# A two-layer interaction network: first tile loaded and multiplied in pieces, first leftovers behind tile 1, layer 2's weights loaded later, matmuls on ones meanwhile

## The chip, the cores and the metric

One core of one Trainium2 chip. The metric is device microseconds of one launch. The kernel before takes 2290.15 us, the median of 3 runs (2289.32 to 2290.17).

## The reference

```python
ROWS, FIELDS, EMB = 4096, 32, 16
def _cin_layer(out, x, W, b, gamma, beta):
    h = jnp.einsum('rne,rfe->rnfe', out, x).reshape(r, -1, e)   # all products of two fields
    h = jnp.einsum('rce,oc->roe', h, W) + b[None, :, None]
    return _batchnorm(h, gamma, beta)                            # statistics over rows and e
h1 = _cin_layer(x, x, W1, b1, g1, beta1)                         # W1: 128 x 1024
out, direct1 = h1[:, :64], h1[:, 64:]
direct2 = _cin_layer(out, x, W2, b2, g2, beta2)                  # W2: 128 x 2048
y = jnp.concatenate([direct1, direct2], axis=1).sum(axis=-1)
```

All in fp32. Layer 2 can't start before the statistics of the whole of layer 1 are there.

## The kernel before

Layer 1 works on 128 tiles of 512 sites. For each tile two factors, a and b (128 x 1024 each, 512 KB), are loaded; VectorE forms four blocks of products, z; TensorE multiplies each with a block of weights. Products that don't fit this pattern ("leftovers", zr, from a load r) serve eight tiles at a time and enter as the first matmuls of every fourth tile. The weights are the sum of two loaded parts. ScalarE evicts, VectorE takes statistics.

```python
w1_sb = wpool.tile([P, 6, P], FP, tag="w1", name="w1_sb")
nc.scalar.dma_start(w1_sb, w1)
w1m_sb = lpool.tile([P, 6, P], FP, tag="a", name="w1m_sb")
nc.scalar.dma_start(w1m_sb, w1m)
bn_sb = load_bn()
w2_sb = const.tile([P, 16, P], FP, tag="w2", name="w2_sb")
nc.scalar.dma_start(w2_sb, w2)                       # 1 MB, used only in layer 2
...
for t in range(NT):
    s = t % GROUP
    if s == 0:
        r = load_rem(t // GROUP)
        zr = rpool.tile([P, T], FP, tag="zr", name="zr")
        nc.vector.tensor_tensor(zr, r[:, :T], r[:, T:], ALU.mult)
    a, b = load_main(t)                              # lpool: three buffers of a and of b
    z = zpool.tile([P, 2, 2, T], FP, tag="z", name="z")     # two buffers
    nc.vector.tensor_tensor(z, a..., b..., ALU.mult)
    if s % 4 == 0:
        for k in range(4):
            ps = pss[t + k] = psum.tile([P, T], FP, tag="ps", name="ps")
            rows = slice(32 * k, 32 * (k + 1))
            nc.tensor.matmul(ps, w1_sb[rows, 4 + s // 4, :], zr[rows, :], start=True, stop=False)
    for m in range(4):
        nc.tensor.matmul(pss[t], w1_sb[:, m, :], z[:, m // 2, m % 2, :], start=False, stop=(m == 3))
    if t > 0:
        finish(t - 1)                                # evictions and statistics
```

A scheduler orders each engine's queue when the kernel is built; it is not always the order of the text.

## Time and profile before

| | before |
|---|---|
| time, median of 6 runs | 2289.79 us |
| first tile's first product on TensorE | 13.41 us |
| eviction of tile 3 | 30.29 us |
| last eviction of layer 1 | 495.34 us |
| TensorE idle between the layers | 16.2 us |

The evictions are the clock by which this study reads layer 1: they come as TensorE finishes a tile. When TensorE never waits, the last eviction comes 465.05 us after tile 3's (495.34 - 30.29), so **any excess over 465.05 is time that TensorE lost after tile 3**.

### The profile page before, as it was taken

The numbers are of one execution on the slowest core, as the hardware profiler recorded it, in microseconds if no ns is written. First come the engines' busy times: TensorE is split into PE (matmuls) and PEld (weight loads), VectorE is DVE, ScalarE is ACT, GpSimd is POOL, SyncE is SP. The second block draws the span as 40 slices with busy tenths as digits, with TensorE's granted clock in tenths as the row PEclk, the third lists the DMA queues.
The fourth block names the chain that finished last, engine by engine and source line by source line (L and its number), as shares of the span: only waits on it lengthen the run. The fifth ranks groups of instructions, "written<-read, shape, count | busy, mean of one in ns | idle before, by whom it ended". The sixth has DMA issues, their size and how long they took to land.

```text
span 2288.8 us, 15238 instructions
## 1 busy us (share of the span) xinstructions
PE 2245.0 (98%) x5376; PEld 982.4 (43%) x5376; DVE 1750.0 (76%) x1129; ACT 398.7 (17%) x580; POOL 2.3 (0%) x5
## 2 busy tenths in 40 slices
PE   8999999979999999999999999999999999999997
PEld 3444444434444444444444444444444444444443
DVE  6888888877777777777777777777777777777776
ACT  3555555556000000000000000000000000000000
POOL 0000000000000000000000000000000000000000
PEclk9999999989999999999999999999999999999998
DMA  8888888868888888888888888888888888888883
GB/s 316 298 305 295 298 292 301 296 201 158 153 150 151 153 154 155 155 150 151 153 157 155 154 150 151 152 158 154 154 150 151 152 159 154 154 149 151 152 155 92
DMA packets 132428, 417.05 MB, mean 182 GB/s; under 512 B 14848, under 2 KB 14848, under 8 KB 115456
## 3 DMA queue, kind: packets, MB, share of 16 engines
q1 hardware_dynamic: 131616, 413.20, 81.7%
q10 hardware_dynamic: 736, 2.89, 0.4%
q8 instruction: 42, 0.69, 0.1%
q14 instruction: 34, 0.28, 0.0%
HBM read 278.66 MB, written 3.15 MB: 123 GB/s over the span
## 4 chain that ended last, share of the span: by engine, by line
PE 77%; issue 22%; DVE 0%; ACT 0%; POOLq 0%; ACTq 0%; DVEq 0%
PE ps L211 77%; ACT h L177 0%; DVE mv L60 0%; POOLq L276 0%; ACTq L182 0%; DVE d L224 0%; DVEq L276 0%; ACT e L213 0%; DVE stats L214 0%; DVE d L215 0%; DVE ss L72 0%; DVE c L69 0%; ACT sd L64 0%; DVE r L66 0%; DVE ss L75 0%
## 5 line engine op out<-in xcount | busy, mean ns | idle before, releaser
L211 PE MATMUL ps<-z,w_sb 128*128 128x512 f32 x4096 | 1761.1, 593 | 16.2 <-ACT h L177 16.2
L208 DVE TENSOR_TENSOR z<-a,b 128x2048 f32<-128x2048 f32 x512 | 1173.0, 2291 | 446.4 <-PE ps L211 439.5
L211 PEld LDWEIGHTS ps<-z,w_sb 128*128 128x128 f32 x4096 | 779.2, 190 | 998.1 <-issue 980.8
L163 PE MATMUL ps<-z,w_sb 128*128 128x512 f32 x1024 | 450.9, 598 | 3.2 <-DVE z L151 3.2
L213 ACT ACTIVATE e<-ps,bn_sb 128x512 f32<-128x512 f32 x128 | 87.9, 687 | 1635.0 <-PE ps L211 1624.0
L151 DVE TENSOR_TENSOR z<-a,b 128x2048 f32<-128x2048 f32 x128 | 293.4, 2292 | 68.9 <-PE ps L163 65.0
L163 PEld LDWEIGHTS ps<-z,w_sb 128*128 128x128 f32 x1024 | 193.0, 191 | 259.6 <-issue 251.0
L129 ACT ACTIVATE e<-ps,bn_sb 128x512 f32<-128x512 f32 x128 | 87.9, 687 | 219.5 <-PE ps L163 219.5
L214 DVE BATCH_NORM_STATS2 stats<-e 128x6 f32<-128x512 f32 x128 | 87.7, 685 | 5.3 <-ACT e L213 5.3
L132 DVE BATCH_NORM_STATS2 stats<-e 128x6 f32<-128x512 f32 x128 | 87.8, 686 | 3.4 <-ACT e L129 3.4
L130 ACT ACTIVATE ed<-ps,bn_sb 64x512 f32<-64x512 f32 x128 | 87.4, 683 | 3.2
L131 ACT ACTIVATE h<-ps,bn_sb 64x512 f32<-64x512 f32 x128 | 87.2, 681 | 2.4
L215 DVE TENSOR_REDUCE d<-e 128x32 f32<-128x512 f32 x128 | 85.5, 668 | 0.0
L177 ACT ACTIVATE h<-h,keep 128x512 f32<-128x512 f32 x64 | 45.7, 800 | 3.8 <-issue 1.9
L161 PE MATMUL ps<-zr,w_sb 32*128 32x512 f32 x256 | 37.4, 655 | 8.1 <-DVE w_sb L115 8.1
L135 DVE TENSOR_REDUCE d<-ed 128x32 f32<-128x512 f32 x64 | 42.8, 668 | 0.0
L161 PEld LDWEIGHTS ps<-zr,w_sb 32*128 32x128 f32 x256 | 10.2, 186 | 31.7 <-issue 23.5
L148 DVE TENSOR_TENSOR zr<-r 128x512 f32<-128x512 f32 x16 | 10.9, 682 | 6.7 <-DMA r<-in_xr 6.7
L60 DVE BATCH_NORM_AGGREGATE mv<-stats 128x2 f32<-128x768 f32 x2 | 7.2, 3612 | 0.0
L129 ACT ACT_TABLE_LOAD x1 | 1.3, 1283 | 8.5 <-DMA bn_sb<-in_bn 8.5
L224 DVE TENSOR_SCALAR d<-d,ss 128x2048 f32<-128x2048 f32 x2 | 2.6, 1343 | 0.0
L180 POOL TENSOR_SCALAR d<-d,direct 128x2048 f32<-128x2048 f32 x1 | 2.0, 2048 | 503.3 <-DVE direct L174 503.3
(17 smaller groups left out, 6.7 us busy)
## 6 DMA issues: line engine op xcount, KB each, us to landing
b<-in_xb SPq DMA_DIRECT2D x128, 1024.0 KB, 7.2
a<-h SPq DMA_DIRECT2D x512, 256.0 KB, 5.2
a<-in_xa SPq DMA_DIRECT2D x128, 512.0 KB, 4.9
b<-in_xb SPq DMA_DIRECT2D x128, 512.0 KB, 5.6
r<-in_xr SPq DMA_DIRECT2D x16, 512.0 KB, 6.1
out<-d SPq DMA_DIRECT2D x2, 1024.0 KB, 4.5
w_sb<-in_w ACTq DMA_DIRECT2D x1, 1024.0 KB, 10.0
out<-d ACTq DMA_DIRECT2D x2, 512.0 KB, 8.9
```

Source lines behind the costliest of these rows:

```text
L129: nc.scalar.activation(e, ps, AF.Identity, bias=b1)
L130: nc.scalar.activation(ed[to, :], ps[KEEP:, :], AF.Identity, bias=b1[KEEP:])
L131: nc.scalar.activation(hs[c][to, :], ps[:KEEP, :], AF.Identity, bias=b1[:KEEP])
L132: nc.vector.bn_stats(stats1[:, t, :], e)
L151: nc.vector.tensor_tensor(z, a.rearrange("p (a t) -> p a t", a=2).unsqueeze(2).to_broadcast([P, 2, 2, T]), b.rearrange("p (b t) -> p b t", ...
L161: nc.tensor.matmul(ps, w1_sb[rows, 4 + s // 4, :], zr[rows, :], start=True, stop=False)
L163: nc.tensor.matmul(pss[t], w1_sb[:, m, :], z[:, m // 2, m % 2, :], start=False, stop=(m == 3))
L208: nc.vector.tensor_tensor(z, a.unsqueeze(1).to_broadcast([P, 4, T]), b, ALU.mult)
L211: nc.tensor.matmul(ps, w2_sb[:, m, :], z[:, k, :], start=(m == 0), stop=(m == 15))
L213: nc.scalar.activation(e, ps, AF.Identity, bias=b2)
L214: nc.vector.bn_stats(stats2[:, t, :], e)
L215: nc.vector.tensor_reduce(d2[half][:, c * RT : (c + 1) * RT], e.rearrange("p (r e) -> p r e", e=EMB), AX.X, ALU.add,)
```

## The change

It is meant to let TensorE start sooner and at full clock: the bytes of the first products come first, and matmuls on ones keep TensorE busy until they land.

```diff
+STARTERS = 3
+LATER = 6
+        ones = zpool.tile([P, 2, 2, T], FP, tag="z", name="ones")[:, 0, 0]
+        nc.vector.memset(ones, 1.0)
+        started = psum.tile([P, T], FP, tag="ps", name="started")
+        for _ in range(STARTERS):
+            nc.tensor.matmul(started, ones[:, :P], ones, start=True, stop=True)
         w1_sb = wpool.tile([P, 6, P], FP, tag="w1", name="w1_sb")
-        nc.scalar.dma_start(w1_sb, w1)
-        w1m_sb = lpool.tile([P, 6, P], FP, tag="a", name="w1m_sb")
-        nc.scalar.dma_start(w1m_sb, w1m)
+        w1m_sb = wpool.tile([P, 6, P], FP, tag="w1m", name="w1m_sb")
+        a0, b0 = factors()
+        load_a(nc.sync, a0, 0, 0, 1)          # first half of a
+        load_b(nc.scalar, b0, 0, 0, 1)        # first half of b
+        load_w1(0, 1)                         # first block of both parts of the weights
+        load_b(nc.sync, b0, 0, 1, 1)
+        load_a(nc.sync, a0, 0, 1, 1)
+        load_w1(1, 6)
...
-        nc.scalar.dma_start(w2_sb, w2)
-        nc.vector.tensor_tensor(w1_sb, w1_sb, w1m_sb, ALU.add)
+        add_w1(0, 1)
...
+            if t == 0:
+                r = load_rem(0)
+                multiply(z, a, b, range(1), range(1));    main(t, z, range(1), True, False)
+                add_w1(1, 6)
+                multiply(z, a, b, range(1), range(1, 2)); main(t, z, range(1, 2), True, False)
+                multiply(z, a, b, range(1, 2), range(2)); main(t, z, range(2, 4), True, False)
+                continue
+            if t == 1:
+                for half in range(2):
+                    multiply(z, a, b, range(half, half + 1), range(2))
+                    main(t, z, range(2 * half, 2 * half + 2), True, False)
+                zr = multiply_rem(r)
+                leftover(0, 2)                # leftovers of tiles 0 to 3, formerly first of all
+                finish(0)
+                continue
...
+            evicted = finish(t - 1)
+            if t == LATER:
+                with tc.issue_after(evicted.ins):
+                    nc.scalar.dma_start(w2_sb, w2)
```

(Cut; some calls are joined on a line. Layer 1's matmuls are also chained in the order of the text, a tile's a and b now stand ahead of r in it, and the second part of the weights, w1m_sb, no longer takes one of the three buffers of a.)

## The prediction

> **What bounds the kernel now.** I read the page's costliest groups first, to learn which engine is never waited out of layer 1.
>
> ```profile
> L163 PE MATMUL ps<-z,w_sb 128*128 128x512 f32 x1024 | 450.9, 598 | 3.2 <-DVE z L151 3.2
> ...
> L151 DVE TENSOR_TENSOR z<-a,b 128x2048 f32<-128x2048 f32 x128 | 293.4, 2292 | 68.9 <-PE ps L163 65.0
> ...
> L161 PE MATMUL ps<-zr,w_sb 32*128 32x512 f32 x256 | 37.4, 655 | 8.1 <-DVE w_sb L115 8.1
> ```
>
> Layer 1's 1024 matmul records waited 3.2 us in all, once, at the start; VectorE waited 65 us for TensorE. So from the first product on, layer 1 is bound by TensorE. Each program matmul is two records, so a tile is 8 records. The timeline of the first 40 us, read second, shows what comes before that steady state, and the evictions (ScalarE, output e) give the pace:
>
> ```profile
> 0.73 0.39 SPq L92 DMA_DIRECT2D r<-in_xr  x1
> 0.74 0.41 ACTq L108 DMA_DIRECT2D w_sb<-in_w  x1
> ...
> 2.14 0.70 ACTq L113 DMA_DIRECT2D w_sb<-in_w  x1
> ...
> 8.14 2.09 PE L161 MATMUL ps<-zr,w_sb 32*128 32x512 f32 x8 [8.14 <-DVE w_sb L115]
> ...
> 11.06 2.29 DVE L151 TENSOR_TENSOR z<-a,b 128x2048 f32<-128x2048 f32 x1 [2.97 <-DMA b<-in_xb]
> ...
> 13.41 16.84 PE L163 MATMUL ps<-z,w_sb 128*128 128x512 f32 x32 [3.17 <-DVE z L151]
> ...
> 17.84 0.34 PEld L163 LDWEIGHTS ps<-z,w_sb 128*128 128x128 f32 x1 [0.52 <-issue]
> 18.69 0.34 PEld L163 LDWEIGHTS ps<-z,w_sb 128*128 128x128 f32 x1 [0.52 <-issue]
> 19.36 0.19 PEld L163 LDWEIGHTS ps<-z,w_sb 128*128 128x128 f32 x1 [0.33 <-issue]
> 19.79 0.19 PEld L163 LDWEIGHTS ps<-z,w_sb 128*128 128x128 f32 x1 [0.24 <-issue]
> ...
> 19.99 0.69 ACT L129 ACTIVATE e<-ps,bn_sb 128x512 f32<-128x512 f32 x1 [10.24 <-PE ps L163]
> ...
> 23.42 0.69 ACT L129 ACTIVATE e<-ps,bn_sb 128x512 f32<-128x512 f32 x1 [1.34 <-PE ps L163]
> ...
> 34.99 0.69 ACT L129 ACTIVATE e<-ps,bn_sb 128x512 f32<-128x512 f32 x1 [2.60 <-PE ps L163]
> ```
>
> Columns are start, duration, engine, and in brackets the idle time before. Four things are to be seen. TensorE does nothing until 8.14 and no product of tile 0 until 13.41, because b lands only at 11.06. Weight loads then come every 0.85 us until about 19.4 and every 0.43 us after it: seven records at half speed, which cost 7 x 0.427 = 3.0 us. Tile 0 is done at 19.97 and tile 1 at 23.40, 3.43 us apart; where a tile has leftovers (30.29 to 34.99) it is 4.70. Last, the evictions of layer 1 end like this:
>
> ```profile
> 495.34 0.69 ACT L129 ACTIVATE e<-ps,bn_sb 128x512 f32<-128x512 f32 x1 [1.34 <-PE ps L163]
> ```
>
> 19.99 + 96 x 3.434 + 31 x 4.70 = 495.4. So nothing but TensorE's own time passes between tile 0 and layer 1's end: whatever TensorE gains by tile 1 should be kept to the end of layer 1, and layer 2 hangs on that end by the batch norm (495.3 to the first matmul at 511.5). Lastly the DMA over the first 12 us, in 40 slices of 0.3 us:
>
> ```profile
> GB/s 0 0 0 0 0 68 109 150 123 246 276 393 393 444 416 396 403 434 440 410 424 435 371 385 494 356 533 410 341 464 478 341 423 437 341 492 410 355 410 410
> ```
>
> Bytes flow from 1.5 us, at about 410 GB/s from 3.3 us: the start is bound by transfers. Summed, 0.66 MB are in by 4.2 us, 1.8 MB by 7.0, 3.4 MB by 10.8. Ahead of b or beside it stood r, both weight sets of layer 1 and the 1 MB of layer 2's weights.
>
> **What the Trainium skill says.** "TensorE: Matmul & The Clock Gate", section "What's actually happening": the array runs at half clock until it has been busy for a whole free-running window of about 3.4 us, and falls back after an idle one. The trace agrees: 0.853 against 0.43 us per record, the fast pace reached 5.9 us after the first product, and layer 2, after 16.2 us idle, starts slow again:
>
> ```profile
> 511.00:512.00 1.00, 0.46 (x1) 0.49 (x2) 0.44 (x1) 1.00 (x3) 0.00 (x0) 0.50 0.83 188
> ...
> 517.00:518.00 1.00, 1.00 (x2) 0.32 (x2) 0.00 (x0) 1.00 (x3) 0.00 (x0) 0.75 0.98 197
> 518.00:519.00 1.00, 1.00 (x4) 0.51 (x3) 0.79 (x1) 1.00 (x3) 0.00 (x0) 1.00 0.72 100
> ```
>
> (Per microsecond, the third column from the end is the granted clock. Around 15 us it reads 1.00, against the matmuls' own pace there; I trust the pace.) "VectorE: DVE Perf Modes", the section on the TRN2 errata: an fp32 product takes (N+151)/0.96 ns; the trace's 2292 ns for N=2048 agrees, so 512 columns cost 0.69 us and 1024 cost 1.22. "DMA: Bandwidth & Descriptors", section "Issuing engines are not separate DMA queues": loads issued from two engines share the same 16 DMA engines. The trace agrees: b waits behind w2 of the other queue. So only the order of the bytes can help, not the second queue.
>
> **The change part by part.**
> 1. *Starters.* VectorE writes ones (about 0.5 us), TensorE multiplies them from about 1.2 us: three matmuls are six records, 6 x 0.853 = 5.1 us at half clock, to about 6.3. They cost nothing while no data are there, and a full busy window should end between 4.6 and 8.0. The cold stretch of tile 0 (3.0 us) goes.
> 2. *Order of bytes.* First come half of a and half of b (0.52 MB) and 0.13 MB of weights: 0.66 MB, in at 4.2, landed by about 4.5. The weights' sum of one block (N=128) is 0.29 us, the first product 0.69, so m=0 could start at 5.5; TensorE is busy with starters to 6.3. The second halves and the other weights make 1.8 MB, about 7.2: sum of 640 columns 0.82 to 8.0, second product 0.69 to 8.7, m=1 to 9.6; third product (1024 columns) 1.22 to 9.9, m=2 and 3 (1.7 us) to 11.7.
> 3. *Tile 1* is the step that sets the gain. Ahead of it lie the 1.8 MB, r (0.52) and its own 1.05: 3.4 MB, 10.8 us, plus 0.5 because loads of before landed somewhat after their byte count: 11.3. Half a product (1.22) to 12.5; from 12.55 TensorE has work all along: 8 records x 0.428 = 3.43 to 16.0, the second half product having ended at 13.8.
> 4. *Leftovers of tiles 0 to 3*, formerly done in dead time at 8.14 to 10.23, now cost 1.14 us plus 0.1 on the busy path: 17.2. Tile 2's a and b (4.46 MB) land about 13.8, its product ends about 16.1 to 16.8, just in time.
> 5. *Layer 2's weights* move behind tile 5's eviction: 1 MB, 2.6 us of transfer, in a stretch that runs at 300 of 410 GB/s with three buffers ahead: hidden. r now queues behind a and b; it has a whole group of 8 tiles in hand later on.
>
> Sum: tiles 0 and 1 and the first leftovers are done at 17.2 instead of 23.4, a gain of 6.2 us: the dead time shrinks by some 4.4 (products 13.41 against an equivalent of 9.0), the cold stretch by 3.0, and the moved leftovers give 1.2 back. The place of the clock's window is chance; the timed runs spread by 0.85 us, and I leave that in the range. 2290.15 - 6.2 = 2283.95, call it 2284.
>
> **Rivals.**
> - *The statistics of tile 0 ahead of tile 2's product on VectorE.* In program order finish(0) now comes before tile 2's product and waits for the leftovers (17.2) and an eviction (0.7). If VectorE's queue keeps that order, the product runs 18.6 to 20.9 and TensorE idles 3.7 us: 2287.7. For it: the text of the change. Against it: before, the program order was the same and the trace has tile 2's product at 19.98 and the statistics at 22.20, so the queue is ordered by readiness.
> - *A start still short of data.* If smaller rows, or more DMAs in flight, slow the transfers by 10%, tile 1 begins 1 us later: 2285. The fifth SyncE load of before was already held 2.2 us for another DMA's completion; fourteen early loads could be held likewise. Conversely, if r is queued behind tile 1's halves, tile 1 comes 1.3 us sooner: 2282.7.
> - *Layer 2's weights collide* with a, b and the next r around 38 us, where DMA is already busy 0.97 of the time, and a product is late by 1 to 2 us: 2285.5. Slack there is about 3 us per load, so I doubt it.
> - *The starters miss the window* or a gap over 3.4 us follows: the cold stretch returns, 2286 to 2287.
> - *All is hidden anyway*, 2290: it would need another bound in layer 1, and 127 evenly spaced evictions speak against it.
>
> **Range and chances.** The gain can't exceed some 9 us (the first data at 4.5 instead of 11.06 and the cold stretch, less the leftovers), which is 0.4%, and no rival loses 45 us. So within 2% is nearly certain. Eight in ten: 2280.5 to 2287.7, from r queued later plus a lucky window to the first rival.
>
> **What would show it right or wrong.** Right: starters from about 1.2 us; tile 0's first record near 6 us; tile 1's records from 12.5 without a gap at 0.43 us each; eviction of tile 0 at 17.2, tile 1's about 2 us (three evictions of 0.7) behind it; tile 2's near 20.7, against 26.85 before; layer 1's last eviction near 489.1. Wrong: weight loads 0.85 us apart after 8 us; tile 2's product behind the statistics; idle time of matmuls on products around tiles 6 to 8; a last eviction whose gain differs from that at tile 2.

## More of the kernel before

```profile
26.97 0.58 SPq L92 DMA_DIRECT2D r<-in_xr  x1
...
30.29 0.69 ACT L129 ACTIVATE e<-ps,bn_sb 128x512 f32<-128x512 f32 x1 [1.34 <-PE ps L163]
...
34.94 0.69 DVE L148 TENSOR_TENSOR zr<-r 128x512 f32<-128x512 f32 x1 [1.18 <-DMA r<-in_xr]
```

The second group's leftovers are needed at tile 8 only, but VectorE takes their product between those of tiles 5 and 6, and waits 1.18 us for r. TensorE doesn't feel it here, but only just: the product of tile 6 ends at 37.83 us (35.55 + 2.28), and TensorE is through with tile 5 at 38.42.

## The result, and the profile after

The changed kernel takes 2289.79 us, the median of 6 runs (2287.66 to 2290.67), and the kernel before 2289.79 in the same rounds: the same. The ratio is 1.000, with a 95% interval of 0.9987 to 1.0012. Ratios here are taken over all fast runs of the same rounds, so not quite the ratio of the medians that are quoted. Executions over 1.5% slower than the fastest of the same kernel are left out of the means. An interval that leaves out 1 tells the two apart, however small the difference.

The page's groups hardly differ; the leftovers no longer wait (8.1 us before), and the tiles' matmuls wait 5.2 us instead of 3.2:

```profile
L198 PE MATMUL ps<-z,w_sb 128*128 128x512 f32 x1024 | 450.9, 598 | 5.2 <-DVE w_sb L134 2.8
L187 DVE TENSOR_TENSOR z<-a,b 128x2048 f32<-128x2048 f32 (+2 forms) x131 | 293.7, 2243 | 68.3 <-PE ps L198 60.0
...
L215 PE MATMUL ps<-zr,w_sb 32*128 32x512 f32 x256 | 36.5, 640 | 0.0
```

The timeline of its first 42 us, with the last eviction of layer 1 added, tells the story:

```profile
1.45 5.49 PE L141 MATMUL started<-ones 128*128 128x512 f32 x6 [1.45 <-DVE ones L138]
...
6.73 1.31 PE L198 MATMUL ps<-z,w_sb 128*128 128x512 f32 x2
...
10.83 4.46 PE L198 MATMUL ps<-z,w_sb 128*128 128x512 f32 x6 [2.79 <-DVE w_sb L134]
...
14.64 2.36 DVE L187 TENSOR_TENSOR z<-a,b 128x1024 f32<-128x1024 f32 x2 [1.98 <-DMA b<-in_xb]
...
15.92 3.70 PE L198 MATMUL ps<-z,w_sb 128*128 128x512 f32 x8 [0.64 <-DVE z L187]
...
27.80 0.69 ACT L170 ACTIVATE e<-ps,bn_sb 128x512 f32<-128x512 f32 x1 [0.89 <-PE ps L198]
...
28.26 0.58 SPq L94 DMA_DIRECT2D r<-in_xr  x1
...
34.75 0.69 DVE L104 TENSOR_TENSOR zr<-r 128x512 f32<-128x512 f32 x1 [3.47 <-DMA r<-in_xr]
...
37.69 7.13 PE L198 MATMUL ps<-z,w_sb 128*128 128x512 f32 x16 [1.80 <-DVE z L187]
...
494.92 0.69 ACT L170 ACTIVATE e<-ps,bn_sb 128x512 f32<-128x512 f32 x1 [1.34 <-PE ps L198]
```

The starters and the first block run nearly where the prediction had them (1.45 and 6.73). Then the start slips: tile 0's second block waits for the weights to 10.83, and tile 1's b lands at 14.64, 3.3 us later than the predicted 11.3. Even so tile 3 is evicted at 27.80, **2.49 us sooner** than before (30.29; one profile each, so to within about 1 us, as the spread below shows). Then VectorE waits 3.47 us for the second group's r, issued later than before (28.26 against 26.97), and now TensorE has nothing in store: it idles 1.80 us at tile 6. The last eviction of layer 1 comes at 494.92, 467.12 after tile 3's: **2.07 us of the 2.49 are lost after tile 3**, all at tile 6 (its eviction comes 5.50 us behind tile 5's, and the spacing is the old one everywhere else). What is left, 0.42 us, is less than the spread of the runs.

Per two microseconds, the busy share of the DMA engines and the GB/s stand last, the granted clock of TensorE ahead of them. The kernel before:

```profile
4.00:6.00 2.00, 0.00 (x0) 0.00 (x0) 0.52 (x1) 0.00 (x0) 0.00 (x0) 1.00 1.03 417
...
8.00:10.00 2.00, 1.86 (x8) 0.51 (x8) 0.09 (x1) 1.28 (x1) 0.00 (x0) 1.00 1.02 422
```

The changed kernel:

```profile
4.00:6.00 2.00, 2.00 (x4) 0.67 (x2) 0.60 (x1) 0.00 (x0) 0.00 (x0) 1.00 0.90 304
...
8.00:10.00 2.00, 0.04 (x1) 0.00 (x0) 1.51 (x3) 1.28 (x1) 0.00 (x0) 1.00 0.99 323
10.00:12.00 2.00, 1.17 (x2) 0.66 (x3) 0.80 (x2) 0.00 (x0) 0.00 (x0) 0.68 0.96 346
12.00:14.00 2.00, 2.00 (x4) 0.85 (x3) 0.67 (x1) 0.00 (x0) 0.00 (x0) 0.50 1.04 420
```

The engines are nearly as busy, but from 4 to 12 us they move 304 to 364 GB/s instead of 401 to 423. And the clock is at half from about 10.8 to 14.2: the starters had raised it (the first block's two records took 1.31 us, against 2.07 without starters in run 9), but after the gap of 2.79 us before the second block it falls again.

### The profile page after: what moved, and what is told of

It reads as the page before. It is cut to its first block, busy times and chain, and to the rows that moved or that the text cites. A ratio compares the mean times of both kernels' runs of the same rounds, so it can differ in the third digit from the quotient of the medians.

```text
span 2288.1 us, 15260 instructions
## 1 busy us (share of the span) xinstructions
PE 2248.7 (98%) x5382; PEld 983.5 (43%) x5382; DVE 1751.8 (77%) x1134; ACT 398.9 (17%) x580; POOL 2.3 (0%) x5
## 4 chain that ended last, share of the span: by engine, by line
PE 77%; issue 22%; DVE 0%; ACT 0%; POOLq 0%; ACTq 0%; DVEq 0%
PE ps L304 77%; ACT h L270 0%; DVE mv L62 0%; POOLq L369 0%; ACTq L275 0%; DVE d L317 0%; DVEq L369 0%; ACT e L306 0%; DVE stats L307 0%; DVE d L308 0%; DVE c L71 0%; DVE ss L74 0%; ACT sd L66 0%; DVE r L68 0%; DVE ss L77 0%
## 5 line engine op out<-in xcount | busy, mean ns | idle before, releaser
L301 DVE TENSOR_TENSOR z<-a,b 128x2048 f32<-128x2048 f32 x512 | 1174.0, 2293 | 445.0 <-PE ps L304 438.1
L187 DVE TENSOR_TENSOR z<-a,b 128x2048 f32<-128x2048 f32 (+2 forms) x131 | 293.7, 2243 | 68.3 <-PE ps L198 60.0
L141 PE MATMUL started<-ones 128*128 128x512 f32 x6 | 5.5, 1088 | 1.4 <-DVE ones L138 1.4
```

Source lines behind the costliest of these rows:

```text
L187: nc.vector.tensor_tensor(z[:, rows.start : rows.stop, cols.start : cols.stop, :], a.rearrange("p (a t) -> p a t", a=2)[:, rows.start : ro ...
L301: nc.vector.tensor_tensor(z, a.unsqueeze(1).to_broadcast([P, 4, T]), b, ALU.mult)
```

## The experiments

Fourteen kernels ran; all gave correct results. The table collects what was read in every trace (us; "lost" is last eviction minus tile 3's, less 465.05). The start of one and the same code varies: five profiles of the changed kernel's start (the changed kernel, runs 1, 5, 6 and 13) have tile 3 at 26.52 to 28.78, and two of the kernel before with the weights later at 27.22 and 28.36. So a single profile tells "lost" well and the start to within about 1 us.

| kernel | tile 3 | lost, and where | last eviction | time (runs) |
|---|---|---|---|---|
| before | 30.29 | 0 | 495.34 | 2289.79 (6) |
| changed | 27.80 | 2.07, tile 6 | 494.92 | 2289.79 (6) |
| 1: leftovers' product later | 26.96 | 1.89, tile 9 | 493.90 | 2288.48 (5) |
| 2: six matmuls on ones | 28.95 | 4.71, tile 6 | 498.71 | 2292.83 (1) |
| 3: as 1, loads whole | 26.59 | 0 | 491.64 | 2287.19 (5) |
| 4: before, w2 behind tile 5 | 28.36 | 1.90, tile 9 | 495.31 | 2289.58 (1) |
| 5: as 1, w2 behind tile 19 | 28.78 | 0 | 493.83 | 2287.53 (5) |
| 6: changed, w2 behind tile 19 | 26.52 | 4.62, tile 6 | 496.19 | 2291.87 (1) |
| 7: before, w2 behind tile 19 | 27.22 | 0.50, tile 23 | 492.77 | 2287.28 (1) |
| 8: combined | 24.76 | 0 | 489.81 | 2284.72 (5) |
| 9: changed, no ones | 27.70 | 2.89, tile 6 | 495.64 | 2291.23 (1) |
| 10: combined, bridge | 24.97 | 0 | 490.02 | 2282.46 (5) |
| 11: as 5, weights whole | 26.45 | 0 | 491.50 | 2286.23 (1) |
| 12: combined, no ones | 26.55 | 0 | 491.60 | 2285.65 (1) |
| 13: as 6, r a tile earlier | 27.72 | 0 | 492.77 | 2287.54 (1) |
| 14: combined, a and b in halves | 25.07 | 0.28, tile 23 | 490.40 | 2284.67 (1) |

**Run 1: the leftovers' product behind tile 7's.** My first theory was that tile 6 is late because VectorE's queue holds it behind a product which only tile 8 needs.

```diff
-                zr = multiply_rem(load_rem(t // GROUP))
+                r = load_rem(t // GROUP)
+                with tc.issue_after(product[-1].ins):     # the z of the tile before
+                    zr = multiply_rem(r)
```

> The changed kernel, with the leftovers' product of each later group ordered behind the product of the tile just before the group; nothing else differs. Theory (the gain of the start is 2.5 us and is given back at tile 6, where VectorE stands in its queue on a load that only tile 8 needs): the start is as in the changed kernel (tile 3's eviction at 27.8, give or take 0.4), TensorE waits less than 0.3 us for products between tiles 4 and 10 (1.8 us in the changed kernel), the last eviction of layer 1 comes at 492.8 instead of 494.92, and the time is about 2 us below the changed kernel's. Rival (tile 6 is late because its own a and b are late, transfers being full, or because layer 2's weights collide): the wait at tile 6 stays at about 1.8 us, now put down to the loads of a or b, and the last eviction stays within 0.5 of 494.9.

The stall at tile 6 is gone, as expected, but another appears at tile 9, 1.89 us, and the last eviction comes at 493.90 instead of 492.8. Its lines in the timeline:

```profile
45.90 2.29 DVE L188 TENSOR_TENSOR z<-a,b 128x2048 f32<-128x2048 f32 x1 [3.92 <-DMA b<-in_xb]
...
48.24 7.99 PE L199 MATMUL ps<-z,w_sb 128*128 128x512 f32 x18 [1.62 <-DVE z L188]
```

A late b, not a late r: the rival about layer 2's weights, wrong for tile 6, was right for tile 9. The time was 2288.48 against 2289.62 of the kernel before, ratio 0.9994 (0.9982 to 1.0007): unresolved by the clock alone.

**Run 2: more ones.**

```diff
-STARTERS = 3
+STARTERS = 6
```

> The changed kernel with six matmuls on ones instead of three: twelve records, seven of them slow to the clock's rise near 7.4 and five fast, to about 9.6, so that only 1.2 us of idle time is left before tile 0's second block at 10.8. Theory (the half clock between 10.8 and 14.2 is not what sets the start, the landing of tile 1's b at 14.6 is): the records of tile 0 after 10.8 come every 0.43 us instead of 0.85, tile 0 is done 1.5 us sooner, but tile 1 still starts near 15.9 and tile 3's eviction stays at 27.8, give or take 0.5. Rival (the cold clock is what eats the gain): tile 1 starts 1.5 us sooner and tile 3's eviction comes near 26.3.

Half right. Tile 0's blocks now ran at full clock (6 records in 2.84 us instead of 4.46), and tile 1 still had to wait for b. But the expectation of 27.8 was missed (28.95): TensorE, done sooner, idled 1.95 us before tile 1, and the clock fell there instead. The same columns of the trace show it:

```profile
14.00:16.00 2.00, 0.62 (x2) 0.38 (x3) 1.90 (x2) 0.00 (x0) 0.00 (x0) 1.00 1.03 422
16.00:18.00 2.00, 2.00 (x4) 0.78 (x3) 1.80 (x2) 0.00 (x0) 0.00 (x0) 0.55 0.89 322
```

So here more ones moved the cold stretch and didn't remove it: the data still came in spurts. At tile 6 the wait was 2.74 us and a further half-clock stretch followed it, hence 4.71 lost.

**Run 3: loads whole.**

```diff
-        load_a(nc.sync, a0, 0, 0, 1)
-        load_b(nc.scalar, b0, 0, 0, 1)
-        load_w1(0, 1)
-        load_b(nc.sync, b0, 0, 1, 1)
-        load_a(nc.sync, a0, 0, 1, 1)
-        load_w1(1, 6)
+        load_a(nc.sync, a0, 0, 0, 2)
+        load_b(nc.scalar, b0, 0, 0, 2)
+        load_w1(0, 6)
```

> As the first of this set, and tile 0's a and b and both parts of layer 1's weights are loaded whole again, in the new order (a and b first, then the weights): 9 early loads instead of 14, rows of 4 KB. Theory (the start is late because the transfers ran at about 300 GB/s over the first 12 us instead of 410, for smaller pieces and loads held back): over 4 to 12 us the transfers reach 400 GB/s or more, tile 1's b lands near 12.3 instead of 14.6, tile 3's eviction comes near 25.5 instead of 27.8, the last eviction near 490.5, and the time is some 4 us below the kernel before. Rival (the pieces are not what slows the start; the first microseconds are slow for any load): tile 1's b lands within 0.7 of 14.6 and the last eviction stays at 492.8, as in the first of this set.

Transfers reached 388 to 420 GB/s between 4 and 12 us, and tile 1's product started at 12.13, as expected:

```profile
12.13 2.36 DVE L185 TENSOR_TENSOR z<-a,b 128x1024 f32<-128x1024 f32 x2 [0.87 <-DMA b<-in_xb]
```

Tile 3 came at 26.59, a microsecond later than expected: about four records of tile 0 still ran at half clock. The gain in time was 2.4 us instead of the expected 4: 2287.19 against 2289.62, ratio 0.9989 (0.9975 to 1.0002).

**Run 4: the kernel before with one part of the change, layer 2's weights behind tile 5's eviction.**

```diff
-        nc.scalar.dma_start(w2_sb, w2)
...
-                finish(t - 1)
+                evicted = finish(t - 1)
+                if t == 6:
+                    with tc.issue_after(evicted.ins):
+                        nc.scalar.dma_start(w2_sb, w2)
```

> The kernel before with one part of the change alone: layer 2's weights loaded behind tile 5's eviction. Theory (much of the start's gain comes from this part, and VectorE's early wait for the second group's leftovers takes it back): tile 0's b lands near 9 instead of 11.06, tile 3's eviction comes near 28 instead of 30.29, then TensorE waits 1.5 to 2 us for a product around tile 6 and the last eviction is back within 0.6 of 495.3. Rival (the wait at tile 6 belongs to the chunks or to the new order of leftovers): no wait there, and the last eviction comes near 493.

The start gained 1.93 us and the end was back at 495.31, as expected; but not at tile 6. It was lost at tile 9, in the way of run 1:

```profile
47.31 2.29 DVE L151 TENSOR_TENSOR z<-a,b 128x2048 f32<-128x2048 f32 x1 [4.48 <-DMA b<-in_xb]
...
49.66 6.70 PE L163 MATMUL ps<-z,w_sb 128*128 128x512 f32 x15 [1.63 <-DVE z L151]
```

My theory of one place fell; there are two. Tile 9's b is issued just ahead of layer 2's 1 MB (35.97 against 36.51), and a load of r passes in the same stretch. In both runs that b takes 11.2 us from issue to landing, where the median of b is 6.1 and 6.9, and three buffers of lookahead didn't cover that. It isn't certain at that place: in run 3, with the 1 MB behind tile 5 too, VectorE waited 1.73 us for tile 9's b and TensorE not at all.

**Runs 5, 6 and 7: the weights halfway between two loads of r**, in run 1's kernel, in the changed kernel and (`t == 20` in run 4's edit) in the kernel before.

```diff
-LATER = 6
+LATER = 20
```

> As the first of the earlier set (the changed kernel with the later groups' leftovers' product behind the product of the tile before), and layer 2's weights loaded behind tile 19's eviction instead of tile 5's, halfway between two loads of leftovers. With TensorE busy throughout, the last eviction comes 465.05 us after tile 3's (30 groups' worth of 4.70 and 3.434, as in the kernel before: 495.34 less 30.29). Theory (the changed kernel gives its gain back at two places: the product of the leftovers that waits for r, and, where that is cured, tile 9's b, which lands late because layer 2's 1 MB and the next r are moved between tiles 6 and 9): tile 9's eviction comes 3.43 us behind tile 8's instead of 5.32, no wait of TensorE for a product between tiles 2 and 40, and last eviction minus tile 3's eviction is 465.1, give or take 0.3; time about 2.5 to 3.3 us below the kernel before. Rival (tile 9 is late for another reason, say the three buffers are drained by the early start whatever else is loaded): tile 9 still comes 5 us behind tile 8 and the difference is 466.5 or more. Second rival (the weights' load costs TensorE 2 us wherever it stands): the stall moves to tiles 21 to 24.

Tile 9 came 3.44 us behind tile 8, nothing was lost after tile 3, and no stall appeared at tiles 21 to 24: the loss at tile 9 was a matter of where the 1 MB stood. Time 2287.53 against 2289.88, the median of eight fast runs before; a ninth (2433.13) doesn't count. Ratio 0.9990 (0.9977 to 1.0003). Its start was the slowest of its kind: it idled 2.80 us before tile 1, and the clock fell there.

> The changed kernel with layer 2's weights behind tile 19's eviction instead of tile 5's, and nothing else. Theory (the stall at tile 6 belongs to the early place of the leftovers' product in VectorE's queue and not to layer 2's weights): TensorE still waits 1.5 to 2.7 us for tile 6's product, put down to VectorE waiting for r, and the last eviction minus tile 3's is 467.1 as in the changed kernel (494.92 less 27.80), give or take 0.5. Rival (the weights' load is what makes r late): no wait at tile 6, difference 465.1.

TensorE still waited at tile 6, so that stall doesn't need layer 2's weights:

```profile
34.37 0.69 DVE L104 TENSOR_TENSOR zr<-r 128x512 f32<-128x512 f32 x1 [4.37 <-DMA r<-in_xr]
...
37.31 8.79 PE L198 MATMUL ps<-z,w_sb 128*128 128x512 f32 x16 [2.70 <-DVE z L187]
```

The total was missed: 4.62 lost instead of 2.07, since the start was sooner by 1.28 us and a half-clock stretch followed the wait.

> The kernel before with layer 2's weights loaded behind tile 19's eviction, and nothing else. Theory: the start is as with the load behind tile 5 (tile 3's eviction at 28.4, give or take 0.5, against 30.29), tile 9 comes 3.43 us behind tile 8, and the last eviction comes at 493.4, so that this small edit keeps 1.9 us. It may lose up to 1 us at tile 5, where VectorE waits for r. Rival (the transfers of layer 1 leave no room for 1 MB more): the gain is lost between tiles 20 and 30 and the last eviction is back at 495.3.

It held in the main: this move alone kept 2.57 us at the end of layer 1 (each end from one profile), and the one run took 2287.28. Nothing was lost at tile 5 or 6. The 0.50 us went at tile 23, where the rival had looked for the loss, but far less than it said; there b took 9.8 us from issue to landing, beside layer 2's weights and the next r:

```profile
96.65 2.29 DVE L151 TENSOR_TENSOR z<-a,b 128x2048 f32<-128x2048 f32 x1 [1.82 <-DMA b<-in_xb]
```

**Run 8: combined.** Loads whole, r behind tile 1's a and b, five matmuls on ones, the leftovers' product behind tile 7's, the weights behind tile 19's eviction. The first, fourth and fifth of these are the edits of runs 3, 1 and 5; the others:

```diff
-STARTERS = 3
+STARTERS = 5
             if t == 0:
-                r = load_rem(0)
...
             if t == 1:
+                r = load_rem(0)
```

> What the runs so far point to: tile 0's a and b and layer 1's weights loaded whole, r behind tile 1's a and b, five matmuls on ones instead of three (ten records, to about 8.3, so that the clock has no idle window before tile 0), the leftovers' product behind the product of the tile before, layer 2's weights behind tile 19's eviction. Theory: tile 0's first record near 9.0, all records 0.43 us apart from there, tiles 0 and 1 and the first leftovers done near 17.2, tile 3's eviction near 24.7 (30.29 in the kernel before, 26.59 in the third run of the earlier set, of which 1.7 is the cold stretch), last eviction near 489.8, time near 2284. Rival (ones make no difference to the clock that the first products see): records 0.85 us apart after 9, tile 3's eviction near 26.3, last eviction 491.4.

Tile 3 at 24.76 and the last eviction at 489.81, as worked out. The sixteen records of tiles 0 and 1 run without a gap at full clock:

```profile
9.45 7.13 PE L196 MATMUL ps<-z,w_sb 128*128 128x512 f32 x16 [1.15 <-DVE w_sb L135]
```

2284.72 us against 2289.88 (the same eight runs as for run 5), ratio 0.9978 (0.9964 to 0.9992).

**Runs 9 and 12: no ones**, in the changed and in the combined kernel.

```diff
-        ones = zpool.tile([P, 2, 2, T], FP, tag="z", name="ones")[:, 0, 0]
-        nc.vector.memset(ones, 1.0)
-        started = psum.tile([P, T], FP, tag="ps", name="started")
-        for _ in range(STARTERS):
-            nc.tensor.matmul(started, ones[:, :P], ones, start=True, stop=True)
```

> The changed kernel without the matmuls on ones. Theory (three matmuls on ones buy nothing, because TensorE idles some 2.8 us between tile 0's first and second block and the clock falls back in the next window): tile 0 still waits for the second weights' sum to 10 to 11, tile 1 still starts within 1 us of 15.9 as its b allows, and tile 3's eviction lies in the span that four profiles of the same start have shown, 26.5 to 28.8 (up to 0.8 more if the clock's window falls badly). Rival (the ones are what the changed kernel gained at the start): tile 3's eviction near 30.

> The combined kernel without the five matmuls on ones. Theory (in the combined kernel TensorE has work without a gap from 9.45, so here the ones are worth the whole cold stretch): records 0.85 us apart from 9.45[...], tile 3's eviction 1.7 to 3.4 us later than 24.76, so 26.5 to 28.2, and last eviction 465.05 behind it. Rival (tile 1's b would set the start anyway): tile 3's eviction within 0.7 of 24.8.

In the changed kernel the ones are worth nothing that shows: tile 3 at 27.70, among the five that have them (26.52 to 28.78, so a worth of under a microsecond could hide there). In the combined kernel they are worth 1.79 us (26.55 against 24.76); the same sixteen records take 8.78 us instead of 7.13:

```profile
9.59 8.78 PE L191 MATMUL ps<-z,w_sb 128*128 128x512 f32 x16 [9.59 <-DVE w_sb L135]
```

Run 9 also lost 2.89 us at tile 6, where TensorE waited 2.62 us; this time the clock held:

```profile
38.42 7.13 PE L193 MATMUL ps<-z,w_sb 128*128 128x512 f32 x16 [2.62 <-DVE z L182]
```

**Run 10: matmuls between the layers.** The combined kernel, with 18 useless matmuls in the 16 us in which TensorE idles between the layers.

```diff
         finish(NT - 1)
+        bridge = psum.tile([P, T], FP, tag="ps", name="bridge")
+        for _ in range(18):
+            with in_order():
+                pe.append(nc.tensor.matmul(bridge, w2_sb[:, 0, :], w2_sb[:, 0:4, :], start=True, stop=True))
```

(Layer 2's first matmul is ordered behind the last of these.)

> The combined kernel, and 18 matmuls without use (layer 2's weights times themselves, the result dropped) between layer 1's last matmul and layer 2's first: 36 records of 0.43 us, 15.4 us of the 16.2 that TensorE idles there. Theory: the clock doesn't fall, so layer 2's first seven records come every 0.43 us instead of 0.85, layer 2 from its first matmul to its last eviction takes near 1758 us instead of 1760.8, the wait before it stays at 16.2, and the time is 2 to 3 us below the combined kernel's 2284.7, near 2282. Rival (the extra matmuls hold up what layer 2 waits for, or the 0.8 us left is enough for the clock to fall): the wait grows by over 1 us, or the first records stay at 0.85, and the time stays at 2284 to 2285.

It held. TensorE's timeline:

```profile
489.82 15.61 PE L263 MATMUL bridge<-w_sb 128*128 128x512 f32 x36
506.29 8.91 PE L309 MATMUL ps<-z,w_sb 128*128 128x512 f32 x20 [0.85 <-DVE z L305]
```

Layer 2's first records no longer run slowly; from its first matmul to its last eviction it takes 1758.28 us (1760.82 in run 8). **2282.46 us against 2289.55, ratio 0.9968 (0.9954 to 0.9981).** The five runs lie within 0.25 us of each other, where the nine of the kernel before spread over 2.2. That the half-clock stretches made the spread fits this, but no run tests it. This is the fastest version, and its interval leaves out 1.

**Run 11: weights whole, a and b still in halves**, as run 5 else.

```diff
-        load_w1(0, 1)
+        load_w1(0, 6)
         load_b(nc.sync, b0, 0, 1, 1)
         load_a(nc.sync, a0, 0, 1, 1)
-        load_w1(1, 6)
```

> As the run with the later leftovers' product and layer 2's weights behind tile 19, with layer 1's two weight loads whole instead of in two pieces each (12 early loads, none held back before tile 1's own a); a and b of tile 0 stay in halves. It tells two readings of the slow start apart. If holding loads back (the second weights were issued near 5.0 to 5.4, after a wait of 2 us) is what costs: 4 to 6 us reaches 390 GB/s or more and tile 1's first product starts near 12.5 instead of 13.4 to 14.6. If the smaller rows cost most: 4 to 8 us stays at 300 to 340 GB/s and tile 1's first product starts between 13.2 and 14.6.

Inconclusive: 362 GB/s in 4 to 6 us and 353 in 6 to 8 lie between the two readings, tile 1's product at 13.30 in the second's range.

**Run 13: r one tile earlier.** After run 12 it was still open why tile 6 suffers in the changed kernel and not before, since VectorE's queue has the same order in both. The queue of loads differs: before, the second group's r stands behind tile 6's a and b; in the changed kernel behind tile 7's, and those wait for a buffer.

```diff
+            if t == GROUP - 1:
+                early = load_rem(1)
+            with tc.issue_after(rems[-1].ins) if t == GROUP - 1 else nullcontext():
+                a, b = (a0, b0) if t == 0 else load_main(t)
```

> The sixth run's kernel (the changed one with layer 2's weights behind tile 19) with one load moved: r of the second group ahead of tile 7's a and b instead of behind them, as the kernel before has it. VectorE's order is as in the changed kernel. Theory (the place of r in the queue of loads is what makes tile 6 late): r is issued near 23 to 24.5 instead of 26.98, VectorE waits for it less than 1.5 us instead of 4.37, TensorE waits less than 0.6 us for tile 6 instead of 2.70, and the last eviction minus tile 3's is 465.1 to 465.7 instead of 469.67. Rival (r lands late wherever it is queued, because transfers are full until 34): TensorE still waits over 1.5 us at tile 6.

That is the cause. Against run 6 this one load moved, and the loss went from 4.62 us to 0 (tile 3 came at 27.72, next to the changed kernel's 27.80, so a later start isn't what spared it):

```profile
23.16 0.58 SPq L96 DMA_DIRECT2D r<-in_xr  x1
...
31.12 0.68 DVE L106 TENSOR_TENSOR zr<-r 128x512 f32<-128x512 f32 x1
```

VectorE doesn't wait for r at all. Counted from tile 3's eviction, r is issued 3.3 us ahead of it in the kernel before and in runs 4 and 7 (26.97, 25.05 and 23.90), 4.6 ahead here, and 0.5 behind it in the changed kernel and run 6. Runs 4 and 7 bear the cause out: their starts were 1.9 and 3.1 us sooner too, r kept its old place, and nothing was lost at tile 6. Not tried: the earlier r with layer 2's weights still behind tile 5, where run 1 lost 1.89 us at tile 9.

**Run 14: halves again, in the combined kernel.**

```diff
-        load_a(nc.sync, a0, 0, 0, 2)
-        load_b(nc.scalar, b0, 0, 0, 2)
+        load_a(nc.sync, a0, 0, 0, 1)
+        load_b(nc.scalar, b0, 0, 0, 1)
         load_w1(0, 6)
+        load_b(nc.sync, b0, 0, 1, 1)
+        load_a(nc.sync, a0, 0, 1, 1)
```

> The combined kernel (eighth run) with tile 0's a and b in halves again, weights whole. If small rows slow the transfers by themselves: 4 to 8 us moves 330 to 365 GB/s with the engines busy all the time, instead of 390 to 405 with whole rows, tile 1's first product starts 0.7 us or more later than the 10.79 of the combined kernel, and tile 3's eviction comes at 25.0 to 26.5 instead of 24.76. If it is only holding back that costs: 4 to 8 us moves 390 GB/s or more and tile 1's first product starts at 10.5 to 11.3.

Halves are slower by themselves (four loads of 256 KB with rows of 2 KB in place of two of 512 KB with rows of 4 KB; which of the two counts isn't separated). Its transfers from 6 to 8 us, then those of the combined kernel:

```profile
6.00:8.00 2.00, 1.76 (x5) 0.46 (x3) 0.71 (x1) 0.00 (x0) 0.00 (x0) 1.00 1.01 354
```

```profile
6.00:8.00 2.00, 2.00 (x6) 0.75 (x4) 1.29 (x2) 0.00 (x0) 0.00 (x0) 1.00 1.04 417
```

The DMA engines are busy all the time in both, yet move 354 instead of 417 GB/s. That stretch shows the most of it; from 4 to 12 us the mean is 375 GB/s against 403. The other runs with whole weights agree: 380 over the same time in run 11 with halves, 398 to 404 in runs 3, 10 and 12 without. Tile 1's product started at 11.81 instead of 10.79. Most of that was won back, because tile 0 starts sooner (8.30 instead of 9.45): the time is about the same, 2284.67 in one run.

## Why the prediction was wrong, point by point

**The bound and the path: right.** Layer 1 is bound by TensorE from tile 1 on; what TensorE has gained by its last tile is what layer 2 gains. Runs 3, 5, 8 and 10 to 13 show the same 465.05 us from tile 3 to the end.

**Part 1, the starters: right up to their end, wrong in what follows.** They ran from 1.45 to 6.94 and raised the clock. I reckoned that the cold stretch then "goes"; I named only "a gap over 3.4 us" as a danger. A gap of 2.79 us was enough, and in this kernel the ones bought nothing that shows (run 9). Run 12 shows what they buy where work follows soon: 1.79 us.

**Parts 2 and 3, the order of the bytes: the term that was mis-sized.** I kept the kernel before's 410 GB/s and its even flow for loads of another shape. The first 12 us brought 3.02 MB (the sum of the six two-microsecond rates times 2 us) where the kernel before had 3.90 MB, so tile 1's b landed at 14.64 instead of 11.3; that 3.3 us is nearly the whole shortfall of the start. With whole loads and r behind tile 1, run 8 brought tile 1's product at 10.79 and the last eviction at 489.81, near the predicted 489.1. Run 14 isolates the halves; loads held back for earlier ones to land (2.1 us at the second weights) add to it in the changed kernel, by an amount that run 11 didn't separate. In place of the predicted 6.2 us the start gained 2.49 in this profile, and 1.5 to 3.8 over the five profiles of this start.

**Part 4, the leftovers: right in kind.** They take 1.14 us on the busy path, and the eviction of tile 0 behind them came at 20.71 instead of 17.2, for part 3's reason. The first rival, VectorE taking the statistics ahead of tile 2's product, didn't happen: tile 2's product ran at 17.20 and the first statistics at 21.90.

**Part 5: the step that failed outright.** "r now queues behind a and b; it has a whole group of 8 tiles in hand later on" is true later on and false for the second group, whose r had about one tile's time. It was issued 1.3 us later than before for a tile that wanted it 2.5 us sooner. It still landed 0.19 us sooner than before (34.75 against 34.94), and the kernel before had 0.59 to spare at tile 6; the other 1.71 of the 2.49 us TensorE had to wait out (it idled 1.80), and with the restart 2.07 us went back. Run 13 shows that r's place in the queue decides it. I had the sentence "whatever TensorE gains by tile 1 should be kept" from evenly spaced evictions. These showed that TensorE hadn't waited, not by how much: VectorE's wait of 1.18 us for r at 34.94 was in the trace, and so was the 0.59 us, where the prediction wrote "Slack there is about 3 us per load". The rival "All is hidden anyway", 2290, was what came; it was put aside on the evenly spaced evictions too. The prediction's own sign of being wrong, idle time around tiles 6 to 8, did appear. Layer 2's weights are not hidden behind tile 5 either (runs 1 and 4: 1.9 us at tile 9, though none in run 3); in the changed kernel itself that loss didn't appear, as tile 6's stall had come first. The rival "layer 2's weights collide" had this mechanism, at the wrong tile.

**The range** ended at 2287.7 because each rival was taken alone, against a sum of 6.2. A start short of data (3.7 of the 6.2 us, in the one profile) together with a stall (2.07) made the whole; that the two medians agree to the hundredth is luck, as the starts alone spread over 2.3 us.

What stays open: why one r of 512 KB takes 6.4 us from issue to landing there (7.9 in the kernel before), while the DMA engines are not always full (279 GB/s from 28 to 32 us).

## What to carry to other kernels

A gain at the start has to be followed to the first place where a load or an in-order queue sets the time: look for waits that the bounding engine doesn't feel yet, and work out how much is to spare (0.59 us here). An earlier start uses it up where the load doesn't move forward with it; where r did (runs 4 and 7), nothing was lost. Put each load by what waits for it, not by its place in the text, and check it in the queues of the built kernel; a large load that isn't urgent belongs where no other extra load passes. Matmuls that only keep the clock up paid here where real work followed without a gap (1.79 us at the start, run 12) and most at the longest idle stretch (between the layers: 2.3 us of the time from run 8 to run 10, taken on different chips, and 2.54 of layer 2 in the traces), not where the data came in spurts.

## What the Trainium skill lacked or had wrong

- "TensorE: Matmul & The Clock Gate", section "Why this matters for your kernels", tells the reader to avoid gaps of over about 3 us, as the clock falls after one idle window. Here it fell after gaps of 1.95 us (run 2), 2.79 (the changed kernel) and 2.80 (run 5), and held after 1.15 (run 8), 1.83 (run 10), 2.33 (the first gap of run 5) and 2.62 (run 9). So shorter gaps can be enough, and their length alone doesn't decide; that it depends on where a gap lies in the window would fit, but no run shows it.
- "DMA: Bandwidth & Descriptors", section "Specifications", gives 512 B as the least transfer for line rate. Loads with rows of 2 KB moved 354 GB/s with the engines fully busy, rows of 4 KB 417 (run 14 against run 8, from 6 to 8 us; 375 against 403 from 4 to 12 us). The number of loads changed too.
- No page that I read has the wait of an early load for the landing of an earlier one that the trace shows (2.1 us at the fifth load of SyncE in the changed kernel, 2.2 us in the kernel before). Whether the chip or the program's own semaphores hold it isn't shown.
